# Four output rows from six input rows, and softmax sums accumulated by transfers: one step of an attention and quantised-convolution kernel

## The chip, the cores and the metric

The kernel runs on one core of one Trainium2 chip. The metric is device time in microseconds. Before the change it is 2024.09 us, the median of three runs (2023.94 to 2026.29).

## What is computed

Sixteen images of 128 channels and 32 x 32 pixels go through an attention layer with four heads and then through two quantised 3x3 convolutions, each with a batch normalisation over all images:

```python
scores = einsum('bnc,bcm->bnm', q, k) * c ** -0.5      # 64 heads (16 images x 4), 1024 x 1024
attn = softmax(scores, axis=-1)
out = einsum('bnm,bmc->bnc', attn, v)                  # then a projection, and + x
x1 = out + x
out = act_quant(x1)                                    # round(clip(x, 0, 1) * 15) / 15
out = conv3x3(out, weight_quant(w1))                   # weights in 15 levels, -7 to 7
out = act_quant(batchnorm(out, gamma1, beta1))
out = conv3x3(out, weight_quant(w2))
result = batchnorm(out, gamma2, beta2) + x1
```

The first convolution of an image can start as soon as that image's attention is done; the second needs the batch statistics of all images. The quantised activations are integers from 0 to 15 and the weights integers from -7 to 7, held in bf16.

## The kernel before, in words

**Stage 1** is one long loop of steps, `NK` = 4 for each of the first 63 heads (index g); the 64th head is done in smaller units, and then comes stage 2. In step (g, k) two blocks of 128 keys are scored against all 1024 queries.

- `scores(g, k)`: four score products, each into one of three PSUM banks (pool `ps_s`), and an exponential by ScalarE from each bank into one of the seven slots of a tile `e` (L551). The pool of `e` has two buffers, so step k + 2 writes into the buffer of step k. VectorE then forms the combinations of a seven-product scheme for the value product: T3 (L554), T1 and T2 (L555) and T4 (L558). T4 is the last of them, and T4 and T3 lie side by side in the tile.
- Then the softmax sums. T4 and T3 of the four steps of a head are added up in a tile `sides[g]` (tag `es`, one buffer, 128 x 1024 f32): at k = 1 the pair of step 0 and that of step 1 (L562), at k = 2 and 3 one more each (L564). All by VectorE.
- `attend(g, k)`, one step later: seven products (psa) from the tile `e`. `evacuate` and `combine` put the four banks together after the head's last step.
- `sum_up(g)` (L625) reduces `sides[g]` across 32-wide blocks, and `normalise(g)` (L652 to L681) makes the inverse sums, spreads them (L664), scales the head's output and adds it to the image's `acc`. After the image's fourth head `acc` is stored to `x1_dram` from SP (L681).
- `project_u` and `project_v` prepare the next head and the next image.

All products go through `product` and the helper `halves` (L403 is the line of all of them): one product is issued as two 64-column halves of the array. An f32 matmul appears as two records in the trace, a bf16 matmul as one.

**The first convolution** of images 0 to 14 is done in the same loop, as a filter that makes two output rows from four input rows (the 15th, the last image, is done directly at the end of the stage). `quantize` writes the image into one of three padded tiles (34 rows of 34, bf16). `transform_rows` (L782) makes four combinations of rows, each of 16 x 34. `rows_product` (psw) multiplies each with three taps: 512 columns, 2 halves, 3 taps, so six matmuls a product and 24 an image; ScalarE copies each product out of the one buffer of `ps_m` (L798), which `project_u` and `project_v` share. `rows_output` (L805, L806, L808) makes the rows of `y`, and `first_statistics` takes its statistics (L298). The images 9 to 14 (`AWAY`) have no room in SBUF until stage 2: their `y` is stored to `y1_dram` from SP (L813), and read back as `back` in one transfer (L987).

**What sets the order.** The program adds functions to a table `later` with the step and half step in which they are traced: `sum_up` of a head at its `end`, `normalise` at `end` + 2, `transform_rows` at `end` + 4, `rows_product` from `end` + 6 to `end` + 8, `rows_output` at `end` + 8. TensorE's order is fixed by `product`, which chains each matmul behind the one before. On the other engines a planner places the instructions at build time by its own estimates of when their inputs are ready, with the traced order as priority; each engine and each queue then runs its list strictly in order. `tc.issue_after(x)` only keeps an instruction behind x on the same engine. Semaphores for every dependence, transfers included, are put in by the framework.

**Stage 2** runs the second convolution on all images, the second statistics, and the output with the residual `res` read back from `x1_dram`.

Of the kernel before, what the change touches and what calls it, by code (L numbers as in the profile page):

```python
# [9 lines left out]
F32 = mybir.dt.float32  # L10
BF16 = mybir.dt.bfloat16
AF = mybir.ActivationFunctionType
ALU = mybir.AluOpType
# [7 lines left out]
ALPHA_EPS = 1e-12  # L21

MAGIC = 12582912.0

# [165 lines left out]
def fast_path(  # L192
# [17 lines left out]
    P = 128  # L210
    B, C, N = x.shape
# [4 lines left out]
    W = 32  # L216
    H = N // W
    NTAP = 9
    RPH = HALF // W
    NPAD = 3  # L220
# [5 lines left out]
    qtp = outer.enter_context(tc.tile_pool(name="qt", bufs=2))  # L226
# [10 lines left out]
    for n in range(2):  # L237
        nc.gpsimd.memset(late[n][:, 0:1], float((B - 1) * N))

    AWAY = range(9, B - 1)  # L240
    ys = [None if b in AWAY else keep.tile([P, N], F32, name=f"y{b}") for b in range(B)]
    pads = []
    for i in range(NPAD):
        t = padp.tile([P, H + 2, W + 2], BF16, name=f"pad{i}")
# [3 lines left out]
    def quantize(b, src, scale, bias, r0=0, r1=H):  # L248

        cut = slice(r0 * W, r1 * W)  # L250
        t = qtp.tile([P, (r1 - r0) * W], F32, tag="qt", name="qt")
        if b == B - 1 and scale == A_LEVELS and r1 == H:
            nc.vector.tensor_scalar(t, src[:, cut], scale, 0.0, ALU.mult, ALU.max)
        else:
            nc.scalar.activation(t, src[:, cut], AF.Relu, bias=bias, scale=scale)
        nc.vector.tensor_scalar(t, t, A_LEVELS, MAGIC, ALU.min, ALU.add)
        return nc.vector.tensor_scalar(
            pads[b % NPAD][:, r0 + 1 : r1 + 1, 1 : W + 1],
            t.rearrange("p (h w) -> p h w", w=W),
            MAGIC,  # L260
            None,
            ALU.subtract,
        )

    def place(n, b, i):
        if b < B - 1:
# [35 lines left out]
    gs = keep.tile([P, 2], F32, name="gs")  # L302
# [7 lines left out]
    ss = keep.tile([P, 2], F32, name="ss")  # L310

    def bn_constants():
        for n, mult in enumerate((A_LEVELS, 1.0)):
            gamma, beta = bnp_sb[:, 2 * n : 2 * n + 1], bnp_sb[:, 2 * n + 1 : 2 * n + 2]
            nc.vector.tensor_scalar(gs[:, n : n + 1], gamma, sc[n], mult, ALU.mult, ALU.mult)
            shift = STEP if n == 0 else 0.0
            nc.vector.tensor_scalar(be[:, n : n + 1], beta, mult, shift, ALU.mult, ALU.add)
            nc.vector.tensor_tensor(ss[:, n : n + 1], sc[n], sc[n], ALU.mult)

    def bn_params(n):  # L320

# [51 lines left out]
    with ExitStack() as ph:  # L373
        pool = lambda name, bufs, **kw: ph.enter_context(tc.tile_pool(name=name, bufs=bufs, **kw))
        once = pool("once", 1)
# [1 line left out]
        up = pool("u", 2)  # L377
        vp = pool("vo", 5)
        ep = pool("e", 2)
        esp = pool("es", 1)  # L380
        avp = pool("av", 1)
        evp = pool("ev", 1)
        smp = pool("small", 4)
# [5 lines left out]
        ps_m = pool("ps_m", 1, space=PSUM)  # L389
# [20 lines left out]
        def halves(out_, lhsT, rhs, start=True, stop=True):  # L410

            for t in (lane[0], 1 - lane[0]):
                done = product(out_[LANES[t]], lhsT(t), rhs, start, stop)
            return done
# [128 lines left out]
        def scores(g, k, between=None):  # L543


            b, h = heads[g]
            e = es[g, k] = ep.tile([P, 7, HALF], F32, tag="e", name=f"e_{g}_{k}")
            for i, (c, m) in enumerate(((0, 1), (1, 1), (0, 0), (1, 0))):
                ps = ps_s.tile([P, HALF], F32, tag="s", name=f"pss_{g}_{k}_{i}")
                score(ps, b, g, k + NK * c, ts(m, HALF))  # L550
                exps[:] = [nc.scalar.activation(e[:, 2 * c + 1 - m], ps, AF.Exp).ins]  # L551
                if between and i in between:
                    between[i]()
            nc.vector.tensor_tensor(e[:, T3], e[:, B12], e[:, B22], ALU.add)  # L554
            nc.vector.tensor_tensor(  # L555
                e[:, T1 : T2 + 1 : T2 - T1], e[:, B12 : B11 + 1], e[:, B11 : T3 + 1 : T3 - B11], ALU.subtract
            )
            nc.vector.tensor_tensor(e[:, T4], e[:, T2], e[:, B21], ALU.add)  # L558
            mine = e[:, T4 : T3 + 1]
            if k == 1:  # L560
                sides[g] = esp.tile([P, NHF, HALF], F32, tag="es", name=f"es_{g}")
                nc.vector.tensor_tensor(sides[g], es[g, 0][:, T4 : T3 + 1], mine, ALU.add)  # L562
            elif k > 1:
                added = nc.vector.tensor_tensor(sides[g], sides[g], mine, ALU.add)  # L564
                sums_added[:] = [added.ins]

        def attend(g, k):
            b, h = heads[g]
# [191 lines left out]

        middle1 = once.tile([P, 2, 3, P], BF16, name="middle1")
        taps1 = wq[0].rearrange("p (y x) o -> p y x o", x=3)
        weights1 = (taps1[:, 0], middle1[:, 0], middle1[:, 1], taps1[:, 2])
        D = H // 2
        FOUR = ((0, 2, ALU.subtract), (1, 2, ALU.add), (2, 1, ALU.subtract), (1, 3, ALU.subtract))
        works, ms = {}, {}

        def transform_weights():  # L770
            with tc.issue_after(sums_added[0]):
                nc.vector.tensor_tensor(middle1[:, 1], taps1[:, 0], taps1[:, 2], ALU.add)
                nc.vector.tensor_tensor(middle1[:, 0], middle1[:, 1], taps1[:, 1], ALU.add)
                nc.vector.tensor_tensor(middle1[:, 1], middle1[:, 1], taps1[:, 1], ALU.subtract)

        def transform_rows(b):
            pad = pads[b % NPAD]
            works[b] = once.tile([P, 4, D, W + 2], BF16, tag="rows", name=f"rows_{b}")
            pick = lambda r: pad[:, r : r + 2 * D - 1 : 2, :]
            for k in (1, 2, 0, 3):  # L780
                x_, y_, op = FOUR[k]
                nc.vector.tensor_tensor(works[b][:, k], pick(x_), pick(y_), op)  # L782

        def rows_product(b, k):
            ps = ps_m.tile([P, D, W], F32, tag="mm", name=f"psw_{b}_{k}")
            for dx in range(3):
                halves(
                    ps,
                    lambda t: weights1[k][:, dx, LANES[t]],
                    works[b][:, k, :, dx : dx + W],  # L790
                    start=(dx == 0),
                    stop=(dx == 2),
                )
            inner = k in (1, 2)
            if k < 2:
                ms[b, inner] = qtp.tile([P, 2, D, W], F32, tag="qt", name=f"m_{b}_{k}")

            nc.scalar.mul(ms[b, inner][:, k // 2], ps, (1.0, 0.5, 0.5, -1.0)[k])  # L798

        def rows_output(b):  # L800
            inner, others = ms.pop((b, True)), ms.pop((b, False))
            if b in AWAY:
                ys[b] = stp.tile([P, N], F32, tag="y", name=f"y_{b}")
            both = once.tile([P, 2, D, W], F32, tag="tiles", name=f"both_{b}")
            nc.vector.tensor_tensor(both[:, 0], inner[:, 0], inner[:, 1], ALU.add)  # L805
            nc.vector.tensor_tensor(both[:, 1], inner[:, 0], inner[:, 1], ALU.subtract)  # L806
            y = ys[b].rearrange("p (i r w) -> p r i w", r=2, w=W)
            nc.vector.tensor_tensor(y, others, both, ALU.add)  # L808

        def first_statistics(b):  # L810
            statistics(b, 0)
# [34 lines left out]
        def at(step, half, fn, *args):  # L846

            later.setdefault(2 * step + half, []).append((fn, args))
# [21 lines left out]
        for g in range(LAST):  # L870
            b, h = heads[g]

            end = (g + 1) * NK
            at(end, 0, sum_up, g)
            at(end, 1, evacuate, g)
            at(end + 1, 0, combine, g, 0)
            at(end + 1, 1, combine, g, 1)
            at(end + 2, 0, combine, g, 2)
            at(end + 2, 1, normalise, g)
            if g > 0:  # L880
                at(g * NK + 1, 0, project_u, g + 1, 0)
                at(g * NK + 2, 0, project_u, g + 1, 1)
            if h == NH - 1:
                at(end + 3, 0, lambda b: quantize(b, accs[b], A_LEVELS, 0.0), b)
                at(end + 3, 1, sums_range, b)
                at(end + 4, 0, transform_rows, b)
                for i, k in enumerate((1, 2, 0, 3)):
                    at(end + 6 + (i + 1) // 2, (i + 1) % 2, rows_product, b, k)
                at(end + 8, 1, rows_output, b)
                at(end + 9, 0, first_statistics, b)  # L890
                if b + 2 < B:
                    at(end + 5, 0, load, b + 2, nc.scalar)
            elif h == NH - 2 and b + 1 < B:

                when = ((4, 0), (4, 1), (6, 1), (7, 0), (7, 1), (8, 0), (8, 1), (9, 1))
                for i, (step, half) in enumerate(when):
                    at(g * NK + step, half, project_v, b + 1, *divmod(i, 2))
# [53 lines left out]
    with ExitStack() as ph:  # L951
# [12 lines left out]
        D = H // 2  # L964
# [385 lines left out]
```

## Time and profile before

| what | value |
|---|---|
| median of three runs | 2024.09 us (2023.94 to 2026.29) |
| profiled execution, span from its first to its last instruction | 2022.7 us (the page gives no other time of it) |
| TensorE / VectorE / ScalarE / GpSimd busy | 98% / 85% / 59% / 1% |
| mean granted TensorE clock | 0.993 |
| stage 1, its last score and value products | until about 1928 us |
| first convolution of 15 images (psw) | 360 matmuls, between 187.7 and 1872 us |
| a head of four steps, e.g. from 1008.71 to 1038.82 us | 30.1 us |
| transfers | 43.74 MB, 22 GB/s over the span |

A line of the groups view gives line, engine, operation, tiles and shapes, the count, then busy time in us and the mean ns of one, then the idle time of the engine ahead of it and what ended most of it. A line of the waits view gives who waited, for whom, the total in us, how often, and the longest. A line of the timeline gives start and length in us, engine, line, operation and tiles, and in brackets the idle time before it and what ended it. `psw` are the products of the first convolution, `pss` the scores, `psa` the value products. A line of the transfers view gives destination and source, the queue, the size in KB, and the median us from issue to landing; a line of its queues gives packets, MB and the time of the packets as a share of 16 transfer engines over the span.

### The profile page before, as it was taken

To read this page: it belongs to the slowest core of one execution; us is meant where nothing else is said; L and a number is where in the kernel's file an instruction comes from. 1 tells how busy PE (TensorE), PEld (TensorE's weight loads), DVE (VectorE), ACT (ScalarE), POOL (GpSimd) and SP (SyncE) were. 2 spreads that over 40 slices of the span, in tenths; PEclk is the share of its full clock that TensorE was granted. 3 is DMA by queue.
4 is the path that set the end of the run, shared out by engine and by line. 5 is a ranking of instruction groups with operands and counts; after the bars stand their busy time and mean duration, and the time that the engine had idled before them with its cause. 6 is when DMAs were issued, how large, how long until landed. Compare 5 with 4: busy or idle time off the path is not lost. (4 is left out here: it accounts for less than half of the span.)

```text
span 2022.7 us, 24701 instructions
## 1 busy us (share of the span) xinstructions
PE 1987.6 (98%) x9497; PEld 730.3 (36%) x9497; DVE 1722.2 (85%) x2642; ACT 1198.5 (59%) x2007; POOL 19.7 (1%) x29
## 2 busy tenths in 40 slices
PE   9999999999999999999999999999999999999994
PEld 3543333333333333333333333433333333333441
DVE  5889888888888888888888888888888888878888
ACT  4565665665566566566556556656656655655575
POOL 0000000000000000000000000000000000000020
PEclk9999999999999999999999999999999999999997
DMA  1000000000000000000000000000000000000064
GB/s 42 24 1 22 1 22 1 22 0 1 22 1 22 1 9 14 0 22 1 21 1 1 22 1 21 11 22 11 1 22 11 22 11 21 11 1 11 11 239 168
DMA packets 12846, 43.74 MB, mean 22 GB/s; under 512 B 1456, under 2 KB 1840, under 8 KB 12720
## 3 DMA queue, kind: packets, MB, share of 16 engines
q1 hardware_dynamic: 9520, 32.05, 4.2%
q10 hardware_dynamic: 3200, 10.03, 1.5%
q8 instruction: 76, 1.25, 0.3%
q14 instruction: 50, 0.41, 0.1%
HBM read 22.16 MB, written 19.92 MB: 21 GB/s over the span
## 5 line engine op out<-in xcount | busy, mean ns | idle before, releaser
L403 PE MATMUL pss<-u,x 128*64 128x512 f32 (+1 forms) x4128 | 1031.9, 589 | 1.6 <-ACT u L509 1.6
L403 PE MATMUL psa<-e,vo 128*64 128x512 f32 (+1 forms) x3624 | 922.4, 588 | 0.0
L551 ACT ACTIVATE e<-pss 128x512 f32<-128x512 f32 x1008 | 595.4, 596 | 380.7 <-PE pss L403 331.9
L403 PEld LDWEIGHTS pss<-u,x 128*64 128x64 f32 x4128 | 351.6, 137 | 549.3 <-issue 493.4
L403 PEld LDWEIGHTS psa<-e,vo 128*64 128x64 f32 x3624 | 304.8, 137 | 483.5 <-issue 449.6
L555 DVE TENSOR_TENSOR e<-e 128x1024 f32<-128x1024 f32 x252 | 307.7, 1221 | 29.8 <-ACT e L551 21.6
L554 DVE TENSOR_TENSOR e<-e 128x512 f32<-128x512 f32 x252 | 172.2, 683 | 105.5 <-ACT e L551 101.7
L558 DVE TENSOR_TENSOR e<-e 128x512 f32<-128x512 f32 x252 | 174.0, 690 | 21.5 <-DVE e L555 0.5
L595 ACT COPY ev<-psa 128x512 f32<-128x512 f32 x252 | 135.5, 589 | 87.2 <-PE psa L403 87.0
L403 PE MATMUL psu<-x,at_sb 128*64 128x512 f32 x512 | 184.9, 599 | 1.0 <-DMA x<-in_x_dram 1.0
L403 PE MATMUL psv<-bt_sb,x 128*64 128x512 f32 x512 | 184.9, 592 | 1.0 <-ACT bt_sb L480 1.0
L530 ACT COPY vo<-psv 128x512 f32<-128x512 f32 x128 | 75.5, 590 | 142.3 <-PE psv L403 142.3
L564 DVE TENSOR_TENSOR es<-es,e 128x1024 f32<-128x1024 f32 x126 | 154.0, 1222 | 2.7
L509 ACT ACTIVATE u<-psu,au_sb 128x512 f32<-128x512 f32 x127 | 87.4, 688 | 21.7 <-PE psu L403 20.1
L798 ACT ACTIVATE m<-psw 128x512 f32<-128x512 f32 x60 | 35.9, 598 | 92.6 <-PE psw L403 90.7
L608 DVE TENSOR_TENSOR y<-ev,y 128x512 f32<-128x512 f32 x63 | 43.6, 692 | 52.4 <-ACT y L606 52.4
L664 DVE STREAM_TRANSPOSE rb<-sums 128x1024 f32<-128x1024 f32 (+1 forms) x66 | 79.8, 1210 | 1.6
L625 DVE TRANSPOSE_TENSOR_REDUCE part<-es 128x32 f32<-128x1024 f32 (+1 forms) x65 | 79.6, 1224 | 1.1
L403 PEld LDWEIGHTS psv<-bt_sb,x 128*64 128x64 f32 x512 | 53.6, 137 | 73.5 <-issue 66.7
L403 PEld LDWEIGHTS psu<-x,at_sb 128*64 128x64 f32 x512 | 53.5, 138 | 73.1 <-issue 69.1
L562 DVE TENSOR_TENSOR es<-e,e 128x1024 f32<-128x1024 f32 x63 | 76.8, 1219 | 0.0
L675 DVE TENSOR_TENSOR av<-av,rb 128x1024 f32<-128x1024 f32 x47 | 57.6, 1225 | 1.6
(159 smaller groups left out, 1193.6 us busy)
## 6 DMA issues: line engine op xcount, KB each, us to landing
x_dram<-acc SPq DMA_DIRECT2D x16, 512.0 KB, 4.3
x<-in_x_dram ACTq DMA_DIRECT2D x15, 512.0 KB, 4.6
res<-x_dram SPq DMA_DIRECT2D x1, 7680.0 KB, 30.0
y_dram<-y SPq DMA_DIRECT2D x6, 512.0 KB, 2.6
back<-y_dram SPq DMA_DIRECT2D x1, 3072.0 KB, 11.4
out_dram<-back SPq DMA_DIRECT2D x6, 512.0 KB, 4.5
out_dram<-y SPq DMA_DIRECT2D x5, 512.0 KB, 4.1
out_dram<-y SPq DMA_DIRECT2D x9, 256.0 KB, 2.5
```

The source lines that it names most:

```text
L403: done = nc.tensor.matmul(out_, lhsT=lhsT, rhs=rhs, start=start, stop=stop)
L509: copied = nc.scalar.activation(dst, ps, AF.Identity, bias=au_sb[:, h : h + 1])
L530: nc.scalar.copy(v[:, c : c + 3 : 2], ps.rearrange("p (h a o) -> p a h o", a=2, o=PH))
L551: exps[:] = [nc.scalar.activation(e[:, 2 * c + 1 - m], ps, AF.Exp).ins]
L554: nc.vector.tensor_tensor(e[:, T3], e[:, B12], e[:, B22], ALU.add)
L555: nc.vector.tensor_tensor(e[:, T1 : T2 + 1 : T2 - T1], e[:, B12 : B11 + 1], e[:, B11 : T3 + 1 : T3 - B11], ALU.subtract)
L558: nc.vector.tensor_tensor(e[:, T4], e[:, T2], e[:, B21], ALU.add)
L562: nc.vector.tensor_tensor(sides[g], es[g, 0][:, T4 : T3 + 1], mine, ALU.add)
L564: added = nc.vector.tensor_tensor(sides[g], sides[g], mine, ALU.add)
L595: nc.scalar.copy(to, ps)
L625: nc.vector.tensor_reduce(part, total.rearrange("p (k c) -> p k c", c=Q), AX.X, ALU.add, apply_transpose=True,)
L664: nc.vector.transpose(rb, rinv.unsqueeze(2).to_broadcast([P, n, Q]))
```

## The change

**The first convolution** of the 15 images makes four output rows from six input rows. `transform_rows` now makes six combinations of 8 x 34 each, in seven VectorE instructions. `rows_product` takes them in three pairs: a pair is two products of 256 columns into the two halves of one bank, so twelve matmuls a pair and 36 an image. ScalarE copies a bank out three times an image. `rows_output` is seven VectorE instructions. Six filter sets are made once, by nine VectorE instructions. All filters carry a common factor 24, so that they stay integers; the last image's quantised values are multiplied by 24 in the same instruction that wrote them, and the batch normalisation constants divide it out again.

**The softmax sums** are no longer VectorE's. At k = 0 a transfer from SP copies T4 and T3 of the step into `sides[g]`; at k = 1, 2 and 3 a transfer issued by GpSimd adds T4 and T3 to it. The tag `es` has two buffers. `sum_up` is traced a step later.

**Room.** Image 8 joins those whose `y` goes through `y1_dram` (seven images).

```diff
-    AWAY = range(9, B - 1)
+    AWAY = range(8, B - 1)
...
+        if b == B - 1:
+            return nc.vector.tensor_scalar(into, t, MAGIC, FACTOR, ALU.subtract, ALU.mult)
...
-        esp = pool("es", 1)
+        esp = pool("es", 2)
...
-            nc.vector.tensor_tensor(e[:, T4], e[:, T2], e[:, B21], ALU.add)
+            last = nc.vector.tensor_tensor(e[:, T4], e[:, T2], e[:, B21], ALU.add)
             mine = e[:, T4 : T3 + 1]
-            if k == 1:
+            sums_added[:] = [last.ins]
+            if k == 0:
                 sides[g] = esp.tile([P, NHF, HALF], F32, tag="es", name=f"es_{g}")
-                nc.vector.tensor_tensor(sides[g], es[g, 0][:, T4 : T3 + 1], mine, ALU.add)
-            elif k > 1:
-                added = nc.vector.tensor_tensor(sides[g], sides[g], mine, ALU.add)
-                sums_added[:] = [added.ins]
+                nc.sync.dma_start(out=sides[g], in_=mine)
+            else:
+                nc.gpsimd.dma_start(out=sides[g], in_=mine, accum_op=ALU.add)
...
         def transform_rows(b):
...
-            works[b] = once.tile([P, 4, D, W + 2], BF16, tag="rows", name=f"rows_{b}")
...
-            for k in (1, 2, 0, 3):
-                x_, y_, op = FOUR[k]
-                nc.vector.tensor_tensor(works[b][:, k], pick(x_), pick(y_), op)
+            works[b] = once.tile([P, 6, D, W + 2], BF16, tag="rows", name=f"rows_{b}")
...
+            nc.vector.tensor_tensor(steps2, pad[:, 2 : H + 2], pad[:, 0:H], ALU.subtract)
+            fused(twos, fours(pad[:, 0:H], 1), -4.0, fours(pad[:, 2 : H + 2], 1))
+            odd, even = twos[:, :, 0:row], twos[:, :, row : 2 * row]
+            nc.vector.tensor_tensor(works[b][:, 2], even, odd, ALU.add)
+            nc.vector.tensor_tensor(works[b][:, 3], even, odd, ALU.subtract)
+            inner = fours(steps2, 1)
+            fused(works[b][:, 4], inner[:, :, 0:row], 2.0, inner[:, :, row:])
+            fused(works[b][:, 5], inner[:, :, 0:row], -2.0, inner[:, :, row:])
+            fused(ends, fours(steps2, 0), -4.0, fours(steps2, 2))
...
+        def rows_product(b, pair):
+            ps = ps_m.tile([P, 2, D, W], F32, tag="mm", name=f"psw_{b}_{pair}")
+            for i, k in enumerate(PAIRS[pair]):
+                for dx in range(3):
+                    halves(
+                        ps[:, i],
+                        lambda t: filters[:, k, dx, LANES[t]],
+                        rows_of(b, k)[:, :, dx : dx + W],
+                        start=(dx == 0),
+                        stop=(dx == 2),
+                    )
...
+            nc.scalar.copy(
+                ms[b, pair // 2 * 2][:, pair % 2], ps.rearrange("p k i w -> p k (i w)")
+            )
...
         def rows_output(b):
...
+            nc.vector.tensor_tensor(both[:, 0], inner[:, :, 0], inner[:, :, 1], ALU.add)
+            nc.vector.tensor_tensor(both[:, 1], inner[:, :, 0], inner[:, :, 1], ALU.subtract)
...
+            fused(y[:, 1], 1, 2.0)
+            fused(y[:, 2], 0, 4.0)
+            nc.vector.tensor_tensor(ends[:, 0], both[:, 0, 0], both[:, 0, 1], ALU.add)
+            nc.vector.scalar_tensor_tensor(
+                ends[:, 1], both[:, 1, 1], 8.0, both[:, 1, 0], ALU.mult, ALU.add
+            )
+            nc.vector.tensor_tensor(
+                y[:, 0:4:3],
+                ends.rearrange("p k (i w) -> p k i w", w=W),
+                outer_.rearrange("p k (i w) -> p k i w", w=W),
+                ALU.add,
+            )
...
-            at(end, 0, sum_up, g)
+            at(end + 1, 0, sum_up, g)
...
-                for i, k in enumerate((1, 2, 0, 3)):
-                    at(end + 6 + (i + 1) // 2, (i + 1) % 2, rows_product, b, k)
+                for i in range(len(PAIRS)):
+                    at(end + 6 + (i + 1) // 2, (i + 1) % 2, rows_product, b, i)
```

In the new code D is 8 (H // 4), and `fused` is a scalar_tensor_tensor: (first input x constant) + second input.

## The prediction

> **What bounds the kernel now.** I read the page's busy shares first, then the groups, the waits, the timelines of one steady head and of one image's first convolution, and the DMA issues.
>
> ```profile
> span 2022.7 us, 24701 instructions
> ...
> PE 1987.6 (98%) x9497; PEld 730.3 (36%) x9497; DVE 1722.2 (85%) x2642; ACT 1198.5 (59%) x2007; POOL 19.7 (1%) x29
> ...
> PE   9999999999999999999999999999999999999994
> ...
> L403 PE MATMUL pss<-u,x 128*64 128x512 f32 (+1 forms) x4128 | 1031.9, 589 | 1.6 <-ACT u L509 1.6
> L403 PE MATMUL psa<-e,vo 128*64 128x512 f32 (+1 forms) x3624 | 922.4, 588 | 0.0
> ...
> L564 DVE TENSOR_TENSOR es<-es,e 128x1024 f32<-128x1024 f32 x126 | 154.0, 1222 | 2.7
> ...
> L562 DVE TENSOR_TENSOR es<-e,e 128x1024 f32<-128x1024 f32 x63 | 76.8, 1219 | 0.0
> ```
>
> TensorE is busy in every slice but the last, and next to nothing releases it late. A busy PE can hide gaps, so I checked by count: between 100 and 1880 us the stretch view has 8111 f32 matmul records and 360 of psw. At the pace of one score step in the timeline (16 records in 1012.14 - 1008.71 = 3.43 us, 0.2144 each) and 0.108 for a psw record (below), that is 1739 + 39 = 1778 of 1780 us. **TensorE is dense; only less work on it, or a new wait of it, moves the time.** VectorE's 85% is second, and costs nothing by itself. Its sums (L562, L564) are 230.8 us.
>
> ```profile
> ACT e L551 <- PE pss L403: 331.9, 662, 3.5
> ...
> ACT e L551 <- DVE es L562: 46.9, 46, 2.7
> ...
> PE pss L403 <- ACT u L509: 1.6, 2, 0.8
> ```
>
> ScalarE waits for the sum L562 because that sum is the last reader of an e buffer (there are two). TensorE doesn't feel it. One case in the timeline:
>
> ```profile
> 1014.67 0.69 DVE L558 TENSOR_TENSOR e<-e 128x512 f32<-128x512 f32 x1
> ...
> 1016.43 1.22 DVE L562 TENSOR_TENSOR es<-e,e 128x1024 f32<-128x1024 f32 x1
> ...
> 1017.75 0.60 ACT L551 ACTIVATE e<-pss 128x512 f32<-128x512 f32 x1 [0.58 <-DVE es L562]
> ```
>
> The exponential starts 0.10 us after the sum ends. The new kernel replaces this reader by a transfer, so **the e buffers are where it can fail**.
>
> **What the Trainium skill says.** (1) "DMA: Bandwidth & Descriptors", SWDGE vs HWDGE vs iDMA: accumulating in a transfer is possible only from GpSimd, whose cores write the descriptors in software; its Specifications give about 1 us to the first byte, against 0.6 from SP and ScalarE. The trace has no GpSimd transfer. (2) The same page, Rules for kernel authors: an accumulate reads its destination and writes it later, so the next one must wait for its semaphore. Hence a head's four transfers form a chain. (3) "SBUF — State Buffer", Who interferes with whom: transfers don't contend with engines, but descriptor writing is locked out while VectorE runs a 2-port copy or tensor_scalar; a tensor_tensor takes only the read side. VectorE's work here is nearly all tensor_tensor, so I expect little of it; no run yet shows it. (4) "TensorE: Matmul & The Clock Gate", LDWEIGHTS: columns / 1.2 ns, so 64 columns are 53 ns; the trace's records last 110 ns (bf16), latency included.
>
> **The change, part by part.**
>
> *TensorE, first convolution.*
>
> ```profile
> 187.66 1.03 PE L403 MATMUL psw<-rows,middle 128*64 128x512 bf16 x5
> 188.32 0.59 PE L403 MATMUL pss<-u,x 128*64 128x512 f32 x1
> 188.53 0.38 PE L403 MATMUL psw<-rows,middle 128*64 128x512 bf16 x1
> ```
>
> The two 64-column halves run side by side. In one half three matmuls of 512 take 188.32 - 187.66 = 0.66 us, 0.218 each. An image has four such products, 12 matmuls a half: 2.62 us. After, it has three pairs of products, 18 matmuls of 256 a half. Half of 0.218 is 0.109. The nearest measured row is
>
> ```profile
> L282 PE MATMUL psc<-pad,wq 128*128 128x256 bf16 x45 | 5.5, 274 | 0.3 <-DVE pad L1007 0.3
> ```
>
> whose 5.5 / 45 = 0.122 contains the tails of groups. So 0.109 to 0.122; I take 0.112, since a new weight load precedes each: 18 x 0.112 = 2.02. Saved: 0.60 us an image, **15 x 0.60 = 9.0 us, all on the path** (0.122 gives 6.4; 0.109 gives 9.9). If the weight loads of both halves serialise beyond the 107 ns that (4) gives for two, say 0.140, only 1.5 us remain. A gain below zero needs 0.146.
>
> *VectorE.* Removed: 230.8 us. Added per image, from rows of before: bf16 tensor_tensor 544 elements 0.436 (L782) and 384 elements 0.35 (L980), so 0.54 ns an element; f32 512 elements 0.69, 1024 1.22; a scalar_tensor_tensor is 0.055 longer (L679, 1.279 against 1.224). No bf16 scalar_tensor_tensor from SBUF is shown: between bf16 speed (0.49 for 544) and f32 speed (0.78); I take the dear end. transform_rows: 0.73 + 0.78 + 2 x 0.29 + 2 x 0.50 + 0.78 = 3.87, for 4 x 0.436 = 1.74. rows_output: 3 x 0.69 + 3 x 0.48 + 0.42 = 3.93, for 2.59. So +3.5 an image (+2.5 at the cheap end), 52 us in all; the filters cost six more instructions once, about 3 us. Net -176 us: VectorE falls to about 77%. Worth nothing on the path, since TensorE covers it, but it brings the sums' inputs T4 forward. *ScalarE*: 45 evacuations of 598 ns for 60, -9 us, hidden too.
>
> *The transfers.* Per head one plain copy from SP and three accumulates from GpSimd, 512 KB each.
>
> ```profile
> q1 hardware_dynamic: 9520, 32.05, 4.2%
> ...
> x_dram<-acc SPq DMA_DIRECT2D x16, 512.0 KB, 4.3
> x<-in_x_dram ACTq DMA_DIRECT2D x15, 512.0 KB, 4.6
> ...
> y_dram<-y SPq DMA_DIRECT2D x6, 512.0 KB, 2.6
> ```
>
> A plain 512 KB lands in 2.6 to 4.6 us; I take 4.5 for the copy. Its packets take 0.042 x 16 x 2022.7 / 9520 = 0.143 us, eight an engine, 1.1 us. An accumulate reads a second stream: +1.1 to +2.2; from GpSimd +0.4 by (1), up to +2 if descriptors are held up. So L, from T4 to landing, is **4.1 (2.6 + 1.1 + 0.4) to 8.8 us (4.6 + 2.2 + 2.0); I take 6.1** (4.5 + 1.1 + 0.4, rounded up).
>
> Is that in time? In the head from 1008.71 to 1038.82 (a period of 30.1 us) T4 ends at 11.94, 15.36, 22.84 and 29.81 (the ends of L558, in us past 1000), and the exponentials that reuse those buffers start at 17.75, 25.50, 33.26 and 40.40. The copy: 11.94 + 4.5 = 16.4, in time. The accumulates, in a chain from 16.4 at the latest: 22.5, 28.9 (from T4 at 22.84), 35.9: all ahead by 3.0 to 4.5 us. With less in front of it on VectorE the first T4 comes sooner and the chain starts at T4 of k = 1. **It fails when 15.36 + 3 L passes 40.40, L = 8.35 us**: then ScalarE waits for the buffer, and TensorE for ScalarE as soon as the three score banks are full. Below that the transfers cost nothing.
>
> *New waits.* SP: the copy waits for T4; behind it stand the x1 and y1 stores, which nobody needs for tens of us. GpSimd: an accumulate waits for T4 and for the one before; behind it stand only accumulates and, near the start, the two maxima of the filters, which themselves wait (L1251 at 56.7 us). I charge 1 us for that start; 0 to 3. VectorE: sum_up, moved a step later, waits for the last accumulate (35.9); behind it in the queue are T4s of later steps. The old order has L625 at 1032.07 and its product L664 is first needed at about 1049, so there are 12 us to spare, and at 77% VectorE has some 7 us idle a head. Nothing charged.
>
> *The end.* A seventh image goes through y1: one store amid the loop, and `back` grows from 3.0 to 3.5 MB, 11.4 to 13.3 us. It is issued at 1928.3, first read at 1951.2; hidden (cover gone: 1.9 us at most). The factor rides in instructions that exist.
>
> **Sum.** Against the profiled execution: 2022.7 - 9.0 + 1.0 = 2014.7 of span. The page gives no other time for it; the runs' median, 2024.1, is 1.4 above its span, which I carry: **2016.1 us**.
>
> **Rivals.** (a) *Weight loads bind the short matmuls.* For it: 110 ns records against 107 ns of streaming, in two halves. Against: a load starts with the matmul before it, and f32 pairs of loads run together. At 0.140 an image saves 0.1 us: 2024.1 - 1.5 + 1.0 = 2023.6, no change. (b) *The accumulates are too long, and the e buffers become the bound.* Place: L551 waiting for a transfer, then pss for L551. From 8.35 us on, each us of L costs 3 us a head, 63 x 3 = 189 us: at L = 9.0, 2016.1 + 123 = 2139 us; at 8.6, 2063. For it: nothing like it has been measured here, and the dear end is 8.8. Against: the sum of measured parts is 6.1. (c) *The sums' cover was worth something too*: ScalarE's 46.9 us of waiting vanish and TensorE gains a few hidden gaps. At most the 2 us of the count: 2016.1 - 2 - 1 (no charge at the start) = 2013.
>
> **How the numbers follow.** The forecast, with (c) as its lower edge, 0.70: 2011 to 2020. (a) or a chain that just eats the gain, 0.08. (b) 0.22, of which about a third lies below 2060. Range 2011 to 2060: about 0.03 below and 0.14 above are left out; the likeliest case alone is 2011 to 2020. A measurement of this kernel tells some 0.2%, 4 us, from no change: faster 0.70, same 0.08, slower 0.22.
>
> **What would show it.** psw: 540 matmuls of 256, about 0.11 us apart in a half; three ScalarE evacuations an image; no L562 and L564, VectorE near 77%; accumulates landing about 6 us after T4; TensorE's slices still at 9, no wait of L551 for a transfer that pss then inherits; period of a head near 30.1 less 0.15. I am wrong if accumulates land later than 8.35 us, or if psw stays 0.14 us apart.

## The result and the profile after

The changed kernel takes **2060.56 us** (median of four runs, 2059.28 to 2061.82), the kernel before beside it 2024.01 us (2022.53 to 2026.29): a ratio of 1.018, with an interval of 1.0167 to 1.0192. It is 36.5 us slower; the forecast was 2016.1. The profiled execution has a span of 2058.9 us (before 2022.7).

First the page of the changed kernel: its span, its busy shares and TensorE's slices, then three of its groups.

```profile
span 2058.9 us, 25656 instructions
...
PE 1999.4 (97%) x9676; PEld 770.2 (37%) x9677; DVE 1526.8 (74%) x2564; ACT 1180.7 (57%) x1992; POOL 183.0 (9%) x218
...
PE   8999999999999999999999999999999999999994
...
L404 PE MATMUL pss<-u,x 128*64 128x512 f32 (+1 forms) x4128 | 1045.1, 591 | 24.2 <-ACT e L552 22.1
...
L566 POOL DMA_DIRECT2D es<-e x189 | 163.4, 865 | 1735.7 <-DVE e L559 1681.7
...
L626 DVE TRANSPOSE_TENSOR_REDUCE part<-es 128x32 f32<-128x1024 f32 (+1 forms) x65 | 79.8, 1228 | 256.4 <-DMA es<-e 256.4
```

VectorE's sums are gone and it is busy 195 us less. But L626, the reduction of a head's sums in `sum_up`, has 256.4 us of idle time ahead of it, all for the transfers; before, this row (L625) had 1.1. The slices of TensorE show next to nothing: 36 us over 40 slices is 2% of each. Its row of score products does: 24.2 us of waiting, 1.6 before. The lines of before to compare with, the group first and then two of its waits:

```profile
L625 DVE TRANSPOSE_TENSOR_REDUCE part<-es 128x32 f32<-128x1024 f32 (+1 forms) x65 | 79.6, 1224 | 1.1
...
ACT ev L615 <- DVE y L613: 23.1, 30, 1.1
...
PEld pss L403 <- ACT e L551: 17.8, 67, 0.7
```

The waits view of the changed kernel shows both ends of the loss, and a link between them:

```profile
DVE part L626 <- DMA es<-e: 256.4, 63, 5.9
...
ACT ev L616 <- DVE y L614: 71.7, 46, 2.3
PEld pss L404 <- ACT e L552: 62.1, 81, 4.3
...
PE pss L404 <- ACT e L552: 22.1, 20, 3.4
```

Once for each of the 63 heads VectorE stands for the last accumulate, 4.1 us on average (256.4 / 63). ScalarE's copy L616 (L615 before, 23.1 us) waits longer for VectorE, and TensorE's weight loads and score products wait for exponentials. The transfers themselves landed inside the estimated range, the copy sooner than estimated; the transfers view of the changed kernel:

```profile
es<-e POOLq DMA_DIRECT2D x189, 512.0 KB, 4.5
es<-e SPq DMA_DIRECT2D x63, 512.0 KB, 2.9
```

How the loss comes about is seen in the timeline of one head that ends in about 1026 us (engines POOL, VectorE, ScalarE and TensorE of the changed kernel, in order of time):

```profile
1019.69 0.69 DVE L559 TENSOR_TENSOR e<-e 128x512 f32<-128x512 f32 x1
...
1020.68 0.86 POOL L566 DMA_DIRECT2D es<-e  x1 [4.90 <-DVE e L559]
...
1025.78 1.25 DVE L626 TRANSPOSE_TENSOR_REDUCE part<-es 128x32 f32<-128x1024 f32 x1 [5.40 <-DMA es<-e]
...
1026.95 0.65 DVE L555 TENSOR_TENSOR e<-e 128x512 f32<-128x512 f32 x1
...
1033.51 3.16 PE L404 MATMUL pss<-u,x 128*64 128x512 f32 x12
...
1034.13 0.62 ACT L613 COPY ev<-y 64x512 f32<-64x512 f32 x1 [1.48 <-DVE y L609]
...
1035.95 0.69 DVE L614 TENSOR_TENSOR y<-y,ev 128x512 f32<-128x512 f32 x1
...
1036.67 0.61 ACT L616 COPY ev<-y 64x512 f32<-64x512 f32 x1 [1.92 <-DVE y L614]
1037.31 1.57 ACT L552 ACTIVATE e<-pss 128x512 f32<-128x512 f32 x3
...
1037.96 1.08 PE L404 MATMUL pss<-u,x 128*64 128x512 f32 x4 [1.29 <-ACT e L552]
```

T4 of the head's last step ends at 1020.38, and GpSimd issues the last accumulate at 1020.68. L626 is the next instruction of VectorE's list, although it is traced a step later: the planner placed it there. (It stands directly behind T4 in 32 of the 63 heads, and a few instructions further back in the others.) It waits 5.40 us. The combinations of the next head's first step (L555) stand behind it, then the whole step that follows is late, L614 with it. ScalarE's copy L616 waits for L614, and **three exponentials that are ready stand behind the copy** (1037.31, x3: the three score banks are full). The twelve score records from 1033.51 take 12 x 0.214 us, to 1036.08; the next start at 1037.96: TensorE lost 1.9 us.

This is no single case. Of the 62.1 us for which weight loads of scores wait for exponentials, 48.9 come behind a copy L616 that had waited for L614, in one unbroken run of ScalarE: 27.5 us in second and 21.4 us in third heads of an image, counted through the whole trace. Before, not one of these waits is of this kind.

I measured the period of a head from one end of the value product to the next in the whole trace. By the head's place in its image (means without the first two images) it was 29.18, 30.11, 28.29 and 31.76 us before, and is 29.18, 31.10, 29.28 and 31.76 now. VectorE's wait at the start of these heads is 3.8, 5.0, 2.5 and 5.0 us. The first and the last head, in which projections of the next image run, absorb it (that the projections are why was not tested); the second and third lose 1.0 each, the second although it holds the shorter convolution.

### The profile page after: what moved, and what is told of

Read it like the earlier page. It is cut to its first block, busy times and chain, and to the rows that moved or that the text cites. A ratio compares the mean times of both kernels' runs of the same rounds, so it can differ in the third digit from the quotient of the medians.

```text
span 2058.9 us, 25656 instructions
## 1 busy us (share of the span) xinstructions
PE 1999.4 (97%) x9676; PEld 770.2 (37%) x9677; DVE 1526.8 (74%) x2564; ACT 1180.7 (57%) x1992; POOL 183.0 (9%) x218
## 5 line engine op out<-in xcount | busy, mean ns | idle before, releaser
L404 PE MATMUL pss<-u,x 128*64 128x512 f32 (+1 forms) x4128 | 1045.1, 591 | 24.2 <-ACT e L552 22.1
L552 ACT ACTIVATE e<-pss 128x512 f32<-128x512 f32 x1008 | 589.0, 596 | 343.8 <-PE pss L404 315.1
L404 PEld LDWEIGHTS pss<-u,x 128*64 128x64 f32 x4128 | 357.8, 137 | 568.5 <-issue 497.2
L404 PEld LDWEIGHTS psa<-e,vo 128*64 128x64 f32 x3624 | 316.3, 137 | 481.7 <-issue 463.2
L556 DVE TENSOR_TENSOR e<-e 128x1024 f32<-128x1024 f32 x252 | 307.4, 1220 | 24.2 <-ACT e L552 14.5
L566 POOL DMA_DIRECT2D es<-e x189 | 163.4, 865 | 1735.7 <-DVE e L559 1681.7
L555 DVE TENSOR_TENSOR e<-e 128x512 f32<-128x512 f32 x252 | 170.6, 677 | 179.7 <-ACT e L552 179.5
L626 DVE TRANSPOSE_TENSOR_REDUCE part<-es 128x32 f32<-128x1024 f32 (+1 forms) x65 | 79.8, 1228 | 256.4 <-DMA es<-e 256.4
L404 PE MATMUL psu<-x,at_sb 128*64 128x512 f32 x512 | 172.5, 597 | 1.4 <-DMA x<-in_x_dram 1.4
L835 ACT COPY m<-psw 128x512 f32<-128x512 f32 x45 | 26.4, 587 | 99.3 <-PE psw L404 98.2
L616 ACT COPY ev<-y 64x512 f32<-64x512 f32 x63 | 38.8, 616 | 72.7 <-DVE y L614 71.7
L404 PEld LDWEIGHTS psu<-x,at_sb 128*64 128x64 f32 x512 | 49.3, 138 | 73.8 <-issue 72.4
L404 PE MATMUL psw<-rows,filters 128*64 128x256 bf16 x540 | 61.5, 278 | 0.0
## 6 DMA issues: line engine op xcount, KB each, us to landing
back<-y_dram SPq DMA_DIRECT2D x1, 3584.0 KB, 12.7
```

The source lines that it names most:

```text
L404: done = nc.tensor.matmul(out_, lhsT=lhsT, rhs=rhs, start=start, stop=stop)
L556: nc.vector.tensor_tensor(e[:, T1 : T2 + 1 : T2 - T1], e[:, B12 : B11 + 1], e[:, B11 : T3 + 1 : T3 - B11], ALU.subtract)
L566: nc.gpsimd.dma_start(out=sides[g], in_=mine, accum_op=ALU.add)
L626: nc.vector.tensor_reduce(part, total.rearrange("p (k c) -> p k c", c=Q), AX.X, ALU.add, apply_transpose=True,)
```

## The experiments

The theory after reading this: **VectorE's list, held by an early wait for a transfer, costs the time, through ScalarE's copies.** The rivals: the transfers' traffic or GpSimd's issuing slows the others; the new convolution costs; VectorE's load as such counts. In what follows, "stands behind" means the order in an engine's list. Line numbers shift by a few between the kernels. The ratio is always against the kernel before, which took 2024.2 to 2025.0 us beside them.

**Each part alone.** e2 keeps the new convolution with the old sums of VectorE; e3 keeps the transfers with the old convolution.

```diff
e2:
-    nc.sync.dma_start(out=sides[g], in_=mine)               (k = 0)
-    nc.gpsimd.dma_start(out=sides[g], in_=mine, accum_op=ALU.add)
+    nc.vector.tensor_tensor(sides[g], es[g, 0][:, T4 : T3 + 1], mine, ALU.add)   (k = 1)
+    added = nc.vector.tensor_tensor(sides[g], sides[g], mine, ALU.add)           (k = 2, 3)
e3: transform_rows, rows_product, rows_output and the filters as before
```

> Only the new first convolution; the sums are VectorE's again, as in the kernel before (one es buffer, sum_up at the head's end). Image 8 still goes through y1. Theory A: TensorE saves 0.6 us an image and nothing else changes, 2013 to 2018 us. Rival (VectorE, now with 52 us more work on top of the sums, becomes late at the head's end): 2022 to 2035 us.

> Only the sums by transfers; the first convolution is that of the kernel before (24 matmuls of 512 an image). Two es buffers, image 8 through y1, sum_up a step later. Theory A: all the loss is here and the convolution's gain is missing, 2065 to 2072 us. Rival (the new transform_rows and rows_output on VectorE contribute to the loss): 2040 to 2058 us.

e2: 2021.89 us, ratio 0.9992 (0.9984 to 1.0). e3: 2059.51 us, ratio 1.0181 (1.0167 to 1.0195), with VectorE waiting 287.5 us for `es`. The whole loss is in the sums, so the convolution is no cause. But alone it gained 2.5 us by the medians, at the edge of what the interval tells from nothing, and not 9; that stays to be explained.

**The reduction further back.** e1 keeps everything and pins L626 behind T4 of the next head's second step; e4 pins it a step earlier, behind the combinations of the next head's first step.

```diff
-    sides[g] = quadrant_sums(...)
+    with tc.issue_after(sums_added[0]):      # e1 and e4
+        sides[g] = quadrant_sums(...)
-    at(end + 1, 0, sum_up, g)                # e4 only
+    at(end, 0, sum_up, g)
```

> The changed kernel, but the reduction of a head's sums (sum_up) is held behind T4 of the next head's second step on VectorE, by which time the last accumulate has landed. Theory A (the 36 us are VectorE standing at sum_up for the transfer, 4.1 us a head, with the next step's combinations queued behind it): the wait of 256 us goes to under 20 us, ScalarE's copy for combine no longer waits, TensorE is dense again, 2014 to 2020 us. Rival B (the accumulates themselves cost the time: e buffers held, descriptors written against VectorE): the order on VectorE doesn't matter, 2055 to 2062 us. Rival C (the 4.8 us of sums now crowd the later steps): between, about 2035 us.

> The changed kernel with one thing moved: the reduction of a head's sums stands in VectorE's list directly behind the combinations of the next head's first step, about half a step to a step later than in the changed kernel, and ahead of the step after that. All transfers stay. If the loss is VectorE standing at the head of its list for the last accumulate (256 us in all), most of that wait lies under the combinations now: under 60 us of it left, no excess of ScalarE's wait for the first run of y (it falls from 72 to under 30 us), and 2015 to 2021 us, that is at or under the unchanged kernel, and lower than e1, which pushed the sums further and crowded them. If the loss is in the transfers themselves (traffic, or GpSimd's issuing, in the way of VectorE), the place of the reduction matters little: 2028 us or more, like e1 or worse.

e1: 2030.38 us (1.0036, 1.0022 to 1.0049). e4: **2016.61 us** (0.9960, 0.9946 to 0.9974), with all 252 transfers as in the changed kernel (landing 4.5 and 2.9 us). In the timeline of e4 the reduction no longer waits:

```profile
1033.39 0.68 DVE L555 TENSOR_TENSOR e<-e 128x512 f32<-128x512 f32 x1
1034.17 1.23 DVE L556 TENSOR_TENSOR e<-e 128x1024 f32<-128x1024 f32 x1
1035.50 0.69 DVE L559 TENSOR_TENSOR e<-e 128x512 f32<-128x512 f32 x1
1036.11 1.24 DVE L626 TRANSPOSE_TENSOR_REDUCE part<-es 128x32 f32<-128x1024 f32 x1
```

and in its waits the other links are gone too:

```profile
ACT ev L616 <- DVE y L614: 29.5, 33, 1.6
...
PEld pss L404 <- ACT e L552: 10.3, 36, 1.3
...
DVE part L626 <- DMA es<-e: 6.2, 4, 5.1
```

So traffic and issuing are not the cause: the same transfers, behind the same instructions, are there at 2016.6 us. Moving one instruction a few places back in VectorE's list (three where it stood directly behind T4) is worth 44 us, with what the planner rearranged around it. e1 removed the wait as well, yet took 14 us more than e4. In e1 the reduction comes a step later, and a new wait appears: the exponentials wait for the transfers that read their `e` buffer. These are the waits of e1:

```profile
POOL es L566 <- DMA es<-e: 155.4, 34, 9.6
...
ACT e L552 <- DMA es<-e: 81.2, 29, 4.6
...
DVE part L626 <- DMA es<-e: 8.0, 1, 8.0
```

GpSimd's accumulates now wait up to 9.6 us for transfers before them, 155.4 us in all (15.6 in the changed kernel): a head's transfers follow each other more closely, and the buffers of `e` come free later. The loss lies in the first head of an image (30.0 us for 29.18), where TensorE's weight loads wait 15.2 us in all for such exponentials. Which part of the planner's new order brings this about I didn't follow.

**No last transfer to wait for.** e5 lets VectorE add the last step's part itself, and two accumulates remain.

```diff
-    else:
+    elif k < NK - 1:
         nc.gpsimd.dma_start(out=sides[g], in_=mine, accum_op=ALU.add)
+    else:
+        nc.vector.tensor_tensor(sides[g], sides[g], mine, ALU.add)
```

> The changed kernel, but the fourth part of a head's sums (k = 3) is added by VectorE, not by an accumulate; two accumulates a head remain, and the last of them has a step's time to land before VectorE reads the tile. Theory A: the wait of VectorE goes (under 30 us in all), though sum_up keeps its early place; 63 additions of 1.22 us come back and are covered: 2014 to 2022 us. Rival B (accumulates cost by themselves): two thirds of the loss stays, about 2045 us.

2018.52 us (0.9971, 0.9962 to 0.9980), VectorE 80% busy, no wait of the reduction: 42 us come back with the reduction left in its early place, directly behind the head's last sum in half of the heads, though VectorE has more to do than in the changed kernel.

**The link through ScalarE, cut.** e14 does nothing to the reduction. It moves ScalarE's second and third copy of `combine` behind the exponentials of the next head's third step; for this, the second part of `combine`, with VectorE's sum of y in it, is traced half a step later.

```diff
-    nc.scalar.copy(s3[BOTTOM], y[TOP])
+    with tc.issue_after(exps[0]):
+        nc.scalar.copy(s3[BOTTOM], y[TOP])
...
-    nc.scalar.copy(sa[BOTTOM], y[BOTTOM])
+    with tc.issue_after(exps[0]):
+        nc.scalar.copy(sa[BOTTOM], y[BOTTOM])
...
-    at(end + 1, 1, combine, g, 1)
+    at(end + 2, 0, combine, g, 1)
```

> The changed kernel with its early reduction of the sums left where it is, so that VectorE still stands there for the last accumulate. Only ScalarE's list is changed: the second and third copies of combine, which wait for VectorE's sums of y, are put behind the four exponentials of the next head's third step instead of ahead of them. If the loss passes through these copies (VectorE late, the copy waits, the exponentials queued behind it come late, the three score banks are full, TensorE stops), most of the 44 us over e4 are gone, although VectorE still waits 150 to 260 us for the transfers: 2016 to 2028 us, score products waiting for exponentials under 20 us. If VectorE's lateness reaches TensorE by another way, such as the value products waiting for the combinations of e, or if it is VectorE's lost time as a whole: 2045 us or more.

2019.83 us (0.9976, 0.9965 to 0.9986). These are its waits (L628 is the reduction, L618 the last copy):

```profile
DVE part L628 <- DMA es<-e: 181.9, 49, 5.9
...
ACT ev L618 <- DVE y L615: 33.5, 63, 2.6
...
PEld pss L404 <- ACT e L552: 3.7, 12, 0.6
```

VectorE still stands 181.9 us for the transfers, and TensorE notices nothing: the head periods are those of e4 (29.18, 29.56, 28.26, 31.76). But the test is clean only in part, because the planner changed VectorE's list too. At the start of 15 of the 16 second heads it put the reduction behind the combinations L556 of the next step, and there the wait went away together with the loss. In the third heads the order of VectorE around the reduction is that of the changed kernel, and the wait is there as before (2.5 us on average in both). VectorE of e14, one second and one third head:

```profile
1005.43 1.22 DVE L556 TENSOR_TENSOR e<-e 128x1024 f32<-128x1024 f32 x1
1006.57 1.24 DVE L628 TRANSPOSE_TENSOR_REDUCE part<-es 128x32 f32<-128x1024 f32 x1
1007.73 0.65 DVE L559 TENSOR_TENSOR e<-e 128x512 f32<-128x512 f32 x1
...
1032.69 1.25 DVE L628 TRANSPOSE_TENSOR_REDUCE part<-es 128x32 f32<-128x1024 f32 x1 [2.29 <-DMA es<-e]
```

So in the third head of an image **a wait of VectorE costs because ScalarE's copies wait for VectorE ahead of exponentials that are ready**, and not by itself: with the copies out of the way the same wait costs nothing. In the second head, that the wait costs is shown by e4 and e5; that it costs through the same copy is read from the traces (the timeline and the count above), and no run cut this link alone.

**A hold without a transfer.** Four more kernels add needless reductions of x (1.22 us each, results unused) to e4: e10 four and e12 three, in a block directly ahead of the next head's first combinations; e11 four, one in each step; e13 three, in a block in a head's fourth step.

```diff
 e = es[g, k] = ep.tile(...)
+if g > 0 and k == 0:                   # e10, e12; e13: k == 3; e11: each k, one
+    for _ in range(4):                 # e12, e13: 3
+        with tc.issue_after(sums_added[0]):
+            quadrant_sums(xt[b])
```

> e4 with four needless reductions of x (1.22 us each, results not used) for each head but the first, on VectorE between the last combinations of a head and the first of the next: where the changed kernel waited for the transfer, VectorE is held 4.9 us (there 4.1 of waiting and 1.2 of reduction). No transfer is added or waited for. If the loss is VectorE being held at this one place, whatever holds it: 25 to 44 us of the 44 between e4 and the changed kernel come back, 2040 to 2060 us, with ScalarE's wait L616 for y (or that of the exponentials' combinations) up again. If it was the transfers' traffic or their late landing: 2016 to 2022.

> The control to e10: the same four needless reductions a head (results not used), one behind each step's combinations, so that VectorE's load is the same, about 91%, but it is held only 1.2 us at a time. If the place counts: well under e10, 2017 to 2030 us. If only the load counts: as e10.

> e10 with three needless reductions instead of four: VectorE is held 3.7 us directly ahead of the next head's first combinations (their results are not used). e10 gave 26 us over e4 for 4.9 us, e11 38 us for the same load spread so that some of it still stood ahead of the value product's combination. If the hold ahead of the combination is what counts: 2026 to 2040 us.

> The same block of three reductions and the same load on VectorE, but directly ahead of the combinations of a head's fourth step, when the head before has been combined and normalised and no copy of ScalarE waits for VectorE. If the place counts: 2016 to 2022 us. If it is VectorE's load, wherever it stands: the time of e12.

Measured, in us: e10 2042.25 (1.0086, 1.0072 to 1.0099), e11 2054.09 (1.0148, 1.0134 to 1.0161), e12 2030.24 (1.0030, 1.0019 to 1.0040), e13 2027.93 (1.0019, 1.0010 to 1.0027). Two of these went against me. e11, which the expectation called the control, is the slowest: some of its reductions stand ahead of the sum of y (L614 in the changed kernel), and in the timeline of one head the same chain runs. VectorE, ScalarE and TensorE of e11:

```profile
1032.72 0.65 DVE L562 TENSOR_TENSOR e<-e 128x512 f32<-128x512 f32 x1
1033.29 0.68 DVE L617 TENSOR_TENSOR y<-y,ev 128x512 f32<-128x512 f32 x1
...
1034.00 0.61 ACT L619 COPY ev<-y 64x512 f32<-64x512 f32 x1 [2.85 <-DVE y L617]
1034.64 1.57 ACT L555 ACTIVATE e<-pss 128x512 f32<-128x512 f32 x3
...
1035.29 1.08 PE L404 MATMUL pss<-u,x 128*64 128x512 f32 x4 [1.86 <-ACT e L555]
```

Here L617 is the sum of y and L619 the copy that waits for it. In all of e11 the reduction waits only 9.1 us for transfers, so it takes hardly any wait for a transfer to stop TensorE in this way; being late when y is due is enough. e13 should have been free and lost 11 us over e4, nearly as much as e12 (14). By head, e13 loses 0.56 us in the second head of an image, which holds the convolution's output rows, and nothing in the third; e12 loses 0.32 and 0.52. My expectation of e13 was wrong about the way: its waits show the same chain again (L618 is the sum of y there, L620 the copy):

```profile
ACT ev L620 <- DVE y L618: 45.3, 36, 2.1
...
PEld pss L404 <- ACT e L556: 24.1, 53, 2.9
```

Of these 24.1 us, 11.7 lie in second heads, 15 times behind a copy L620 that had waited. So y came late there too; how a block in a head's fourth step delays it, I didn't follow. The planner ordered the rest anew in each build (e10 loses 1.43 in the second head and 0.08 in the third), so I draw no slope from these four, and no rule on where a hold is free.

**Where the convolution's gain was.** e9 is the missing corner: old convolution, and the transfers with the reduction placed as in e4 (the edits of e3 and e4 together).

> The old convolution, the sums added by transfers, and the reduction of a head's sums behind the next head's first combinations as in e4: the corner that was missing beside the kernel before (2024.2), the new convolution alone (e2, 2021.9) and both with the reduction well placed (e4, 2016.6). If the two parts are independent, this is 2024.2 - 7.6 + 2.5 = 2019.1. If the transfers are worth nothing by themselves and only let the new convolution show its predicted 9 us (VectorE at 86% swallowed the rest in e2): 2023 to 2025. If the transfers cost time wherever they are waited for: over 2026.

2025.64 us (1.0003, 0.9996 to 1.0009).

| | sums on VectorE | sums by transfers, reduction as in e4 |
|---|---|---|
| old convolution | 1 (before) | 1.0003 (e9) |
| new convolution | 0.9992 (e2) | 0.9960 (e4) |

The two parts aren't additive. The transfers alone are worth nothing (the head periods of e9 are those of before to 0.01 us). With them the convolution brings 0.0043 x 2024 = 8.7 us, near its predicted 9.0; without them 0.0008 x 2024 = 1.6 (2.5 by the medians). The intervals leave the size of this difference open: it is 7 us here, and 4 with e7 and e8 (below) in the places of e2 and e4. The traces show the difference itself without that noise. In e2 VectorE is busy 86%, and the head with the products takes 29.82 us, in e4 29.56, before and in e9 30.11: a gain of 0.29 us an image without the transfers, 0.55 with them.

Where the other half goes in e2, its trace points to: in the second heads weight loads wait 7.4 us in all, 15 times, for exponentials that had waited for VectorE's sum L563, the last reader of their `e` buffer. Before, no weight load waits in these heads for such an exponential. No run cut this wait alone.

**The filters.** The nine VectorE instructions that make the filters come as one block near step 7. e6, e7 and e8 are e5, e2 and e4 with one of them per step.

```diff
-    at(NK + 3, 1, transform_weights)
+    for i in range(9):
+        at(NK + 4 + i, 1, transform_weights, i)      # the i-th instruction alone
```

> e5 (last sum by VectorE) with the nine instructions that make the filters put one to a step over nine steps, not all at one half step. If they, as one block on VectorE at a point where ScalarE and TensorE wait for its combinations, cost the 2.2 us that the ends of the third head show, this takes about 2 us off e5: 2016.5. If those 2 us are only VectorE's work at the start whatever its place, no difference: 2018.5.

> e2 (new convolution, sums all by VectorE) with the nine filter instructions spread one to a step. The predicted gain of the convolution was 9 us and e2 showed 2.5. If the block of filter instructions is 2.2 of what is missing: 2019.7 us. If not: 2021.9. The remaining 4 us would lie in the images' products themselves either way.

> e4 with the nine filter instructions spread one to a step: all of the change kept, with both of its misplaced pieces of VectorE work moved. If both readings hold: 2 us under e4, 2013 to 2019 us, and the least of all. If the accumulates as such cost time wherever they are waited for: above e6.

e6 2015.87 (0.9963, 0.9949 to 0.9976), e7 2021.19 (0.9983, 0.9977 to 0.9990), e8 2017.78 (0.9966, 0.9952 to 0.9979). Against their partners: -2.7, -0.7 and +1.2 us, with overlapping intervals each time, so these times don't tell what the block costs. The traces do, for the third head of the run, where the block stands: 31.02 and 31.10 us with it in e5 and e2, 28.88 and 28.85 without it in e6 and e7. In e4, where the reduction is pinned, 29.61 with and 29.50 without (e8). It is a loss of some 2 us, once, and not in every build. e4, e6 and e8 are the best versions, and these runs don't rank them; all beat both kernels, by 6 to 9 us and by 43 to 45 us.

## Why the prediction was wrong

**The step that failed** is the one on new waits, where it says of VectorE: "sum_up, moved a step later, waits for the last accumulate (35.9); behind it in the queue are T4s of later steps", and then "there are 12 us to spare", "some 7 us idle a head. Nothing charged." Three things in it were wrong. It took the traced position for the position in the list; the planner kept the reduction at the end of the head, in half of the heads directly behind T4, where VectorE then waits 4.1 us a head. It measured the spare time of the reduction's own consumer (the product L664), and not that of what stands behind it in the list: the combinations, and through them y. And the 7 us of idle time a head are an average, which lies elsewhere. The charge should have been 44 us (the changed kernel less e4). That it is this wait, e4 and e5 show by removing it. That it costs through ScalarE's copies, e14 shows for the third head of an image and the traces for the second.

**The rival named for the other side, (b), didn't happen.** It had the accumulates so long that the exponentials wait for an `e` buffer. Its 2063 us for 8.6 us a transfer is near the measured time by chance only. They landed in 4.5 us, and the changed kernel's waits have no row of L552 for a transfer of any size. It cost something in e1 alone (81.2 us, where the reduction was pushed too far back); in the other kernels with transfers it is at most one wait, of up to 4.3 us.

**TensorE dense, so only a new wait moves the time:** right, and it is how the loss was found.

**The products at 0.112 us, 0.60 us an image, 9.0 us in all:** right in size. In the timeline of the changed kernel one group of products shows the pace:

```profile
1046.88 0.88 PE L404 MATMUL psw<-rows,filters 128*64 128x256 bf16 x9
1047.54 0.59 PE L404 MATMUL psa<-e,vo 128*64 128x512 f32 x1
1047.60 0.50 PE L404 MATMUL psw<-rows,filters 128*64 128x256 bf16 x3
```

The first half's six start at 1046.88 and psa takes this half at 1047.54: 0.110 each, and not the 0.140 of rival (a). The head with the products went from 30.11 to 29.56 us in e4, 0.55. What the step lacked is its condition: "all on the path" held only with VectorE relieved of the sums. In e2, where it keeps them and gets the transforms as well, about half of the gain in that head is lost.

**VectorE at 77%, worth nothing by itself:** 74% measured (the transforms and output rows came to 3.6 and 3.7 us an image by their mean durations, for 3.87 and 3.93), and e9 confirms "nothing" for the relief alone. It wasn't quite so with the new convolution: there it is what lets the whole gain through. Rival (c), up to 3 us more from the relief alone, is refuted by e9.

**The transfers at 6.1 us from T4:** in the case above T4 ends at 1020.38 and the reduction starts 5.40 later; over the 63 heads the median is 4.9. Inside the range of 4.1 to 8.8, and it didn't decide. **The end:** `back` took 12.7 us for the 13.3 estimated. **ScalarE:** 45 evacuations of 587 ns are 26.4 us, 9.5 less, as said.

With its reduction put behind the next step's combinations the change gives 2016.6 us, and the prediction said 2016.1. That these two agree to half a microsecond is partly luck: the interval of e4 is 2.8 us wide to each side, and the 1 us for the start was never measured by itself. But the large term of its sum, the convolution, had its size (8.7 us for 9.0, with VectorE relieved); the one missing term was an instruction that waits in an ordered list.

## What to carry to other kernels

When work leaves an engine for a transfer, the engine that waits for the transfer gets a new instruction that can block its list: ask what stands behind that instruction and who waits for that, not when its own result is needed, and pin its place instead of trusting the order in which it was traced. An idle share is no slack at a place, least of all ahead of copies that sit in front of another engine's urgent work. Where one part of a change takes from an engine what another part gives to it, measure all four corners: here the two gains did not add.

## What the runs showed of the hardware

In the changed kernel a 512 KB accumulating transfer within SBUF lands 4.5 us (median) after its issue, a plain one of the same size from SP 2.9, and GpSimd is occupied 0.865 us for each accumulate. I had feared that VectorE's work holds up GpSimd's descriptors; in the 252 transfers of the changed kernel the landing stayed between 2.8 and 6.3 us, with VectorE busy 74%. The bf16 scalar_tensor_tensor from SBUF ran at the pace of f32: 272 and 544 elements took 0.43 and 0.72 us, a f32 one of 256 elements 0.42, while a bf16 tensor_tensor of 1088 took 0.72.
